# Cross-attention with image prompts: values projected with their weights standing, turned into row groups by VectorE, and some small work moved off VectorE

## The chip, the cores and the metric

The kernel runs on one core of a Trainium2 chip. The metric is the device time of one execution, in microseconds (us); lower is better. Engines are called as in the profile: PE is TensorE (matmuls; PEld its weight loads), DVE is VectorE, ACT is ScalarE, POOL is GpSimd, and SP is SyncE, which here only issues DMAs. All data is 32-bit floating point.

## What is computed

For each of 8 batches, 112 queries attend in 20 heads of 16 channels to a context of 371 text tokens and 4 image prompt tokens, each of 512 channels. The reference, cut to what matters (`heads` splits 320 channels into 20 heads of 16):

```python
q = heads(x @ W_q)                      # 8 x 20 x 112 x 16
k_t = heads(text @ W_k)                 # text: 371 tokens of 512
v_t = heads(text @ W_v)
probs_t = softmax(q @ k_t.T * 0.25)
text_out = probs_t @ v_t
k_ip, v_ip = heads(ip @ W_k_ip), heads(ip @ W_v_ip)   # 4 prompt tokens
qsem = l2norm(probs_t @ text)           # per head, 512 wide
sem = qsem @ l2norm(ip).T
probs_ip = softmax(q @ k_ip.T * 0.25 + 0.5 * sem) * spatial_mask
out = (text_out + probs_ip @ v_ip) @ W_out + b_out + x
```

The kernel never forms `qsem`. It forms the Gram matrix of the context (tokens by tokens, with the normalised prompts as further columns), and multiplies the exponentials of each head by a matrix `u` whose columns are the doubled upper half of that Gram matrix, the products with the prompts, a column of ones, and the 16 value channels of the head. One product thus gives the norm of `qsem`, the four similarities, the softmax's sum and the head's text output.

## The kernel before

The 20 heads are worked in 5 groups of 4; a step (b, g) is one group of one batch, and there are 40 steps. Group 0 to 3 take heads out of the first two chunks of 128 channels (a chunk holds 8 heads), group 4 the four heads of the last 64 channels. The four heads of a group lie in the four row groups of 32 partitions of TensorE, so that four small products run side by side.

In step n the main loop (lines 1253 to 1337) does the following, in an order written out by hand for TensorE, VectorE and SP throughout, and for ScalarE too in the main loop; GpSimd is ordered by the planner until near the end.
- `scores` (line 692) of the group two steps ahead (`LEAD = 2`): two heads at the start of the step, two behind the fifth block of the product. The scores go to two banks of PSUM (`ps_sc`, two buffers), so the later two need the banks of the earlier two. `maxima` (line 721, DVE) and `exponentials` (line 733, ACT, which for b > 0 also copies the four prompt logits, line 740) read them; `sent` (line 742) issues a DMA on SP that moves the probabilities of a head into the ring tile `xg`.
- `turned` (line 747): VectorE transposes `xg` of the next step in 32x32 blocks into `xgT`, in two pieces of 1024 and 512 elements.
- `multiplied` (line 760): the product of the current step, 12 blocks of 32 tokens times four heads, into four banks (`ps_qd`).
- `value_sums` (line 783, ACT) and `reduced` (line 815, DVE) read the four banks.
- `placed` (line 664, POOL) writes the values of the next step's heads into the value columns of `u`, from the tile `vr`.
- `between` (line 1113): pieces of other work that fill TensorE behind the product: `gram`, `values`, `keys`, `project_queries` for the coming batches, and `finish` of the last one (lines 836 to 960), which ends with the residual sum (line 955, DVE, out of PSUM) and the output DMA.

Values and keys of batch b + 1 are made during batch b. `values` (line 591) takes the context (`ctxT`, embedding by tokens) as the standing operand and the value weights as the moving one: three chunks of 128 tokens, each four matmuls of 320 columns, or of 384 for batches 1 to 6, where the 64 columns of the keys' third chunk are appended to the weights (line 1193). Each chunk is copied out by ScalarE into `vext` (tokens by channels). `regrouped` (line 614) then copies 16 blocks of 32 partitions into `vr`, whose row group a holds head a's values for all tokens; ScalarE and GpSimd do this in steps (b, 3) and (b, 4) (lines 1266 to 1270, 1324). `order_values` (line 252) has first put the weights' columns in the order that this needs. `keys` (line 546) keeps the weights standing and moves 371 columns of `ctxT` per chunk, which gives channels by tokens. The third chunk of keys is projected like that for batch 0 and, in `last_keys` (line 575), for batch 7, in step (7, 1); for batches 1 to 6 the 64 appended columns are spread by GpSimd (line 608) into `k3` and turned by three TensorE transposes (line 556) in step (b, 4). In the third chunk only every other block of 16 channels holds a head; the blocks between are zero (`spread`, line 139, does this to the weights).

`project_queries` (line 345) transposes x on VectorE, multiplies, and writes each chunk twice, times one of two masks that keep every other head (line 378): on VectorE, but for one chunk on ScalarE.

In the prologue (lines 1168 to 1217) the first context is transposed on TensorE (`transposed_context`, line 414, copied out by ScalarE, the second of three chunks by VectorE), the prompts are normalised on VectorE, and batch 0's keys and values, its first two groups' scores, the first chunk of batch 1's values and the loads of batch 2's context follow.

The last batch has a loop of its own (lines 1348 to 1405). In it GpSimd too is in written order: the bias sum of batch 6 (`with_bias`, line 832), which needs a load of x issued at the end of step (6, 4) (line 1230), stands ahead of `placed` for group 1.

Of the kernel before, what the change touches and what calls it, by code (L numbers as in the profile page):

```python
# [14 lines left out]
NIP = 4  # L15
# [5 lines left out]
def kernel(  # L21
# [83 lines left out]
    wv_sb = const.tile([P, NE, C + REST], F32, tag="wv_sb", name="wv_sb")  # L105
# [79 lines left out]
    wv_in = work.tile([P, BLK, P], F32, tag="xgT", name="wv_in")  # L185
    wv_in = wv_in.rearrange("p j k -> p (j k)")[:, : NE * C].rearrange("p (e f) -> p e f", f=C)
# [8 lines left out]
    load_embed(nc.sync, wv_in, w_v)  # L195
# [39 lines left out]
    k3 = const.tile([P, NT, GROUP, 2, D], F32, tag="k3", name="k3")  # L235

    def more_constants():
        nc.gpsimd.memset(k3[:, :, :, 1, :], 0.0)
# [6 lines left out]
    kip = const.tile([P, NC, N], F32, tag="kip", name="kip")  # L245
# [5 lines left out]

    def order_values():

        wv_by = wv_sb[:, :, :C].rearrange("p e (a g d) -> p e a g d", g=NG, d=D)
        for i in range(FULL):
            nc.vector.tensor_copy(
                wv_by[:, :, :, 2 * i : 2 * i + 2, :],
                wv_in[:, :, i * P : (i + 1) * P].rearrange("p e (a r d) -> p e a r d", r=2, d=D),
            )
        nc.vector.tensor_copy(  # L260
            wv_by[:, :, :, 2 * FULL, :],
            wv_in[:, :, FULL * P :].rearrange("p e (a d) -> p e a d", d=D),
        )
# [30 lines left out]
    def prompt_projections():  # L294

        both = work.tile([2 * N, CP], F32, tag="ipkv", name="ipkv", bufs=1)
        kp = both[:N]
        last = kp[:, FULL * P :].rearrange("n (a r d) -> n a r d", r=2, d=D)
# [28 lines left out]
        nc.scalar.copy(kip, ps[:, : NC * N].rearrange("p (i n) -> p i n", n=N))  # L327
        nc.gpsimd.tensor_copy(st[1]["kT"][:, :, TT:], kip[:, :, NIP : 2 * NIP])
        for i in range(NC):
            nc.gpsimd.tensor_tensor(  # L330
                kipb[:, i],
                kip[:, i, :NIP].unsqueeze(1).to_broadcast([P, HC, NIP]),
# [12 lines left out]
    def project_queries(bs):  # L345
# [16 lines left out]
        for i in range(NC):  # L362
# [13 lines left out]
            for r in range(2 if i < FULL else 1):  # L376
                by = nc.scalar.mul if (bs[0], i) == (1, 1) else nc.vector.tensor_scalar_mul
# [8 lines left out]
    def begin(b):  # L386
# [5 lines left out]
        s["kT"] = work.tile([P, NC, T], F32, tag="kT", name=f"kT_{b}")  # L392
        s["k3"] = k3
        s["u"] = work.tile([P, UCOL], F32, tag="u", name=f"u_{b}")
        s["vr"] = work.tile([P, BLK, NG, D], F32, tag="vr", name=f"vr_{b}")
# [1082 lines left out]
```

## Time and profile before

| | |
|---|---|
| time, median of 3 runs (lowest, highest) | 411.79 us (411.24, 412.38) |
| time of the profiled execution | 411.79 us |
| its span | 410.1 us |
| mean granted TensorE clock | 0.999 |
| busy ACT, POOL | 218.9 us (53%), 130.1 us (32%) |
| `ps_qd` matmuls, line 773 | 216.2 us, 3840 records |
| `ps_s`, line 702 | 65.3 us, 320 records |
| `ps_v`, line 599 | 63.1 us, 192 records |
| `ps_k`, line 565 | 46.6 us, 136 records |
| DVE transposes of probabilities, line 754 | 126.1 us, 79 |

A line of a timeline reads: start in us, duration in us, engine, line of the kernel, operation, output<-inputs by the program's names, shapes, and how many were merged (x2); in square brackets how long the engine had been idle ahead of it, and which instruction ended that. Merged pieces may overlap on the page, because an instruction's record is longer than the time until the next one starts. A line of the chain reads: start, us, engine, output tile, line, records. A matmul of 32-bit data leaves two records. A group's line reads: line, engine, operation, names and shapes, count, then busy us, mean ns of one, and the idle time ahead of the group with what ended it.

### The profile page before, as it was taken

The page shows a single profiled execution, that of the slowest core. Times are in us where ns is not written, and L with a number is a line of the kernel's source. Part 1 is how long each engine was busy: PE and PEld are TensorE (multiplying, and loading weights), DVE is VectorE, ACT ScalarE, POOL GpSimd, SP SyncE. Part 2 cuts the span into 40 slices and gives each one's busy share as a digit, 9 for nine tenths or more (in the row PEclk, how much of TensorE's full clock was granted, in tenths as well). Part 3 has the DMA queues.
Part 4 walks back from the last instruction along what each step waited for, and adds up shares of the span by engine and source line. Part 5 has one row for each costly group of instructions (what it writes and reads, how often), then busy time and mean ns, then how long its engine had stood idle before and what let it go on. Part 6 is the DMA issues. An engine that isn't in the chain of part 4 may idle for free.

```text
span 410.1 us, 14107 instructions
## 1 busy us (share of the span) xinstructions
PE 404.9 (99%) x5476; PEld 317.6 (77%) x5476; DVE 341.6 (83%) x734; ACT 218.9 (53%) x732; POOL 130.1 (32%) x321
## 2 busy tenths in 40 slices
PE   8999999999999999999999999999999999999996
PEld 7767777887778867888777877778777987787893
DVE  5667788897999979898899988889798977889775
ACT  2563345636375544646256363644537453678773
POOL 4842113021171204412052120702126121544640
PEclk9999999999999999999999999999999999999999
DMA  7575666548644555456554555545444356544300
GB/s 222 155 195 118 219 157 153 152 122 202 164 128 127 151 138 136 119 138 177 146 137 118 159 147 135 152 110 164 127 126 106 105 169 159 128 122 132 109 5 29
DMA packets 46435, 56.95 MB, mean 139 GB/s; under 512 B 9405, under 2 KB 40961, under 8 KB 46368
## 3 DMA queue, kind: packets, MB, share of 16 engines
q1 hardware_dynamic: 46328, 55.99, 51.3%
q8 instruction: 43, 0.70, 0.7%
q14 instruction: 24, 0.20, 0.2%
q10 hardware_dynamic: 40, 0.07, 0.1%
HBM read 15.88 MB, written 1.39 MB: 42 GB/s over the span
## 4 chain that ended last, share of the span: by engine, by line
PE 96%; DMA 1%; DVE 1%; issue 0%; ACT 0%; POOL 0%; SPq 0%; POOLq 0%
PE ps_qd L773 42%; PE ps_v L599 15%; PE ps_k L565 11%; PE ps_s L702 11%; PE ps_g L515 7%; PE ps_q L368 4%; PE ps_o L989 3%; DMA ct<-in_ctx_dram 1%; PE ps_g L471 1%; PE ps_o L944 1%; PE ps_k L581 1%; PE ps_k L556 0%; PE ps_a L977 0%; DVE ipnT L269 0%; PE ps_ipkv L306 0%
## 5 line engine op out<-in xcount | busy, mean ns | idle before, releaser
L773 PE MATMUL ps_qd<-u,xgT 32*112 32x168 f32 (+11 forms) x3840 | 216.2, 350 | 0.0
L773 PEld LDWEIGHTS ps_qd<-u,xgT 32*112 32x112 f32 x3840 | 184.4, 172 | 25.3 <-issue 0.5
L738 ACT ACTIVATE p<-ps_s,nmx 112x371 f32<-112x371 f32 x156 | 84.3, 578 | 81.5 <-DVE nmx L724 75.4
L754 DVE STREAM_TRANSPOSE xgT<-xg 128x512 f32<-128x512 f32 (+2 forms) x79 | 126.1, 1604 | 1.0 <-DMA ct<-in_ctx_dram 1.0
L724 DVE TENSOR_REDUCE nmx<-ps_s 112x1 f32<-112x371 f32 x160 | 78.8, 536 | 25.6 <-PE ps_s L702 24.4
L819 DVE CUSTOM_DVE_ANT_0 junk<-ps_qd,p 112x371 f32<-112x371 f32 x146 | 79.2, 543 | 19.1 <-ACT pvs L786 3.6
L671 POOL COPY u<-vr 128x64 f32<-128x64 f32 x120 | 26.4, 238 | 138.3 <-PE ps_qd L773 103.4
L702 PE MATMUL ps_s<-kT,qm 32*112 32x375 f32 (+1 forms) x320 | 65.3, 495 | 0.0
L599 PE MATMUL ps_v<-wv_sb,ctxT 128*128 128x384 f32 (+1 forms) x192 | 63.1, 477 | 0.0
L599 PEld LDWEIGHTS ps_v<-wv_sb,ctxT 128*128 128x128 f32 x192 | 35.7, 190 | 21.9 <-DVE qm L378 0.5
L565 PE MATMUL ps_k<-ctxT,wk_sb 128*128 128x371 f32 x136 | 46.6, 487 | 0.0
L702 PEld LDWEIGHTS ps_s<-kT,qm 32*112 32x112 f32 x320 | 25.4, 171 | 12.8 <-issue 10.3
L565 PEld LDWEIGHTS ps_k<-ctxT,wk_sb 128*128 128x128 f32 x136 | 24.5, 189 | 13.5 <-ACT vext L606 0.2
L619 ACT COPY vr<-vext 32x240 f32<-32x240 f32 x88 | 34.2, 389 | 1.3
L606 ACT COPY vext<-ps_v 128x384 f32<-128x384 f32 (+1 forms) x24 | 11.2, 467 | 41.3 <-PE ps_v L599 41.3
L515 PE MATMUL ps_g<-ctxT 128*32 128x375 f32 (+11 forms) x672 | 30.4, 333 | 0.0
L515 PEld LDWEIGHTS ps_g<-ctxT 128*32 128x32 f32 x672 | 27.7, 110 | 2.0
L422 DVE STREAM_TRANSPOSE ctxT<-ct 128x512 f32<-128x512 f32 x21 | 22.9, 1104 | 3.4 <-DMA ct<-in_ctx_dram 3.2
L964 POOL TENSOR_TENSOR wv<-vip,w 112x1280 f32<-112x1280 f32 x6 | 14.8, 2465 | 26.7 <-DVE w L902 26.7
L740 ACT COPY ipl<-ps_s 112x4 f32<-112x4 f32 x140 | 23.0, 164 | 0.0
L487 ACT ACTIVATE ug<-ps_g 128x375 f32<-128x375 f32 (+2 forms) x24 | 8.3, 375 | 24.1 <-PE ps_g L515 10.5
L488 POOL TENSOR_TENSOR ug<-ug,half 128x128 f32<-128x128 f32 (+1 forms) x24 | 10.4, 447 | 26.4 <-ACT ug L487 26.4
(171 smaller groups left out, 343.0 us busy)
## 6 DMA issues: line engine op xcount, KB each, us to landing
xg<-p SPq DMA_DIRECT2D x156, 162.3 KB
u<-ug SPq DMA_DIRECT2D x122, 99.0 KB
ct<-in_ctx_dram SPq DMA_DIRECT2D x28, 176.0 KB
vip<-vipd SPq DMA_DIRECT2D x6, 560.0 KB
xr_sb<-in_x_dram SPq DMA_DIRECT2D x32, 35.0 KB
out_dram<-ob SPq DMA_DIRECT2D x8, 140.0 KB
x_sb<-in_x_dram SPq DMA_DIRECT2D x6, 140.0 KB
xg<-wv_sb SPq DMA_DIRECT2D x4, 162.3 KB
```

The lines of the kernel that those rows point to most:

```text
L515: nc.tensor.matmul(ps[c][q * RG : (q + 1) * RG, j * RG - c * P : T - c * P], ctxT[:, e, j * RG : (j + 1) * RG], ctxT[:, e, j * RG : T], st ...
L565: nc.tensor.matmul(ps[:, :TT], wk_sb[:, e, i * P : (i + 1) * P], s["ctxT"][:, e, :TT], start=(e == 0), stop=(e == NE - 1),)
L599: nc.tensor.matmul(ps[:, :w], ctxT[:, e, c * P : (c + 1) * P], wv_sb[:, e, :w], start=(e == 0), stop=(e == NE - 1),)
L619: copy(s["vr"][a * RG : (a + 1) * RG, q::QN].rearrange("p c g d -> p c (g d)"), s["vext"][q * RG : (q + 1) * RG, :, a * w : (a + 1) * w],)
L671: nc.gpsimd.tensor_copy(v, dealt(b, c, s["vr"][:, c * QN : (c + 1) * QN, g, :]))
L702: nc.tensor.matmul(ps[:S, :w], qm[a * RG : (a + 1) * RG, i, r, j * S : (j + 1) * S], s["kT"][a * RG : (a + 1) * RG, i, :w], start=True, st ...
L724: nc.vector.tensor_reduce(nmx, s["sc", g, a][:S, :TT], AX.X, ALU.max, negate=True)
L738: nc.scalar.activation(s["p", g][:, a, :], ps[:S, :TT], AF.Exp, bias=nmx)
L740: nc.scalar.copy(s["ipl"][:, groups[g][a], :], ps[:S, TT:T])
L754: nc.vector.transpose(xT[:, j0:j1].rearrange("p j (k q) -> p q j k", q=QN), xg[:, :, j0 * RG : j1 * RG].rearrange("p q (j k) -> p q j k", ...
L773: nc.tensor.matmul(banks[a][:S, j * RG : UW], xT[a * RG : (a + 1) * RG, j, :S], region(b, c)[a * RG : (a + 1) * RG, q, j * RG - c * P :], ...
L819: nc.vector.tensor_tensor_reduce(out=junk, in0=ps[:S, :TT], in1=s["p", g][:, a, :], scale=1.0, scalar=0.0, op0=ALU.mult, op1=ALU.add, accu ...
```

## The change

- `values` now works as `keys` does: the value weights stand, 371 columns of context move, for the first two chunks of 128 channels. ScalarE copies a chunk into the new tile `vT` (channels by tokens).
- The value weights' last 64 columns go where the zeros stood in the keys' third chunk (`spread` with `other`); the third chunk is projected in full for every batch, and its rows hold keys and values in turn. The queries are zero in the rows of values, since their weights and masks are.
- `values_to_groups` has VectorE transpose a chunk in 32x32 blocks straight into `vr`: chunk 1 at the end of step (b, 0), the third chunk and the next batch's chunk 0 at the end of (b, 1); for batch 7 the third chunk and chunk 1 at the end of (6, 2) and (6, 3). `regrouped`, `order_values`, `k3`, the TensorE transposes of keys and `last_keys` are gone.
- `kT` has columns up to 384, and the prompts' keys `kip` are padded with zeros to 13 per batch.
- Batch 7's third chunk of keys moves from step (7, 1) to (6, 1), and one of its chunks of values from (6, 1) to (6, 2).
- The query masks go to ScalarE, except batch 0's and the last chunk of batch 7's. The residual of batches 0 to 5 becomes a ScalarE copy out of PSUM and a GpSimd sum.
- In the prologue the first context's copies are halved and all on ScalarE, the normalised prompts come one place later in part, and the loads of batch 2's context come earlier on SP.

```diff
-    wv_sb = const.tile([P, NE, C + REST], F32, tag="wv_sb", name="wv_sb")
+    wv_all = const.tile([P, NE * CP], F32, tag="wv_sb", name="wv_sb")
+    wv_sb = wv_all[:, : NE * C].rearrange("p (e f) -> p e f", f=C)
...
-    def spread(eng, t):
+    def spread(eng, t, other=None):
...
-        eng.memset(v[:, :, :, 1, :], 0.0)
+        if other is None:
+            eng.memset(v[:, :, :, 1, :], 0.0)
+        else:
+            eng.tensor_copy(
+                v[:, :, :, 1, :], other[:, :, FULL * P :].rearrange("p k (a d) -> p k a d", d=D)
+            )
...
+    vT = const.tile([P, FULL, TP], F32, tag="vT", name="vT")
+    nc.gpsimd.memset(vT[:, :, TT:], 0.0)
...
-                by = nc.scalar.mul if (bs[0], i) == (1, 1) else nc.vector.tensor_scalar_mul
+                by = nc.vector.tensor_scalar_mul
+                if qT is None and not (end and i == FULL):
+                    by = nc.scalar.mul
                 by(qm[:, i, r, : n * S], ps[:, : n * S], emask[:, r : r + 1])
...
+        n = NE // 2
         for c in range(NT):
...
+            for k in range(0, NE, n):
+                ps = bank(f"ps_c_{b}_{c}_{k}", spare=c == NT - 1)
+                for e in range(k, k + n):
...
+                nc.scalar.copy(
+                    ctxT[:, k : k + n, c * P : c * P + rows],
+                    ps[:, : n * P].rearrange("p (e t) -> p e t", t=P)[:, :, :rows],
                 )
...
+    def projected(ps, w, i, ctxT):
+
+        for e in range(NE):
+            nc.tensor.matmul(
+                ps[:, :TT],
+                w[:, e, i * P : (i + 1) * P],
+                ctxT[:, e, :TT],
+                start=(e == 0),
+                stop=(e == NE - 1),
+            )
+
     def keys(b):
...
+        for i in range(NC) if b < B - 1 else (FULL, 0, 1):
+            ps = bank(f"ps_k_{b}_{i}")
+            projected(ps, wk_sb, i, s["ctxT"])
             nc.scalar.copy(s["kT"][:, i, :TT], ps[:, :TT])
             yield
...
     def values(b):
...
+        for i in range(FULL):
+            ps = bank(f"ps_v_{b}_{i}")
+            projected(ps, wv_sb, i, st[b]["ctxT"])
+            nc.scalar.copy(vT[:, i, :TT], ps[:, :TT])
             yield
...
+    def values_to_groups(b, i):
+
+        src = vT[:, i] if i < FULL else st[b]["kT"][:, FULL]
+        nc.vector.transpose(
+            st[b]["vr"][:, :, 2 * i : 2 * i + 2].rearrange("p j r d -> p j (r d)"),
+            src.rearrange("p (j t) -> p j t", t=RG),
+        )
...
-        nc.vector.tensor_tensor(ob, s["o"][:S, :C], s["xb"], ALU.add)
+        if bd is None:
+            nc.scalar.copy(ob, s["o"][:S, :C])
+            eng.tensor_tensor(ob, ob, s["xb"], ALU.add)
+        else:
+            nc.vector.tensor_tensor(ob, s["o"][:S, :C], s["xb"], ALU.add)
...
         if g == 0:
+            values_to_groups(b, 1)
...
-            run(("v", nb), lambda: values(nb), 2)
+            run(("v", nb), lambda: values(nb), 2 if nb < B - 1 else 1)
+            if nb == B - 1:
+                run(("k", nb), lambda: keys(nb))
...
-            else:
-                run(("k", nb), lambda: keys(nb))
-            run(("v", nb), None)
+            run(("k", nb), lambda: keys(nb), 2 if 0 < b and nb < B - 1 else 1)
+            if nb == B - 1:
+                run(("v", nb), None)
...
+        if (b, g) in ((B - 2, 2), (B - 2, 3)):
+            values_to_groups(nb, FULL if g == 2 else 1)
+        if g == 1:
+            values_to_groups(b, FULL)
+            values_to_groups(nb, 0)
...
-            if nb < B - 1:
-                run(("k", nb), None, 1)
...
+    load_ctx_blocks(LEAD, rest=False)
     for a in range(GROUP):
         scores(0, 0, a, early=True)
         probabilities(0, 0, a)
...
-    load_ctx_blocks(LEAD, rest=False)
     spread(nc.gpsimd, wq_sb)
-    nc.gpsimd.tensor_copy(wv_sb[:, :, C:], wk_sb[:, :, FULL * P : C])
-    spread(nc.gpsimd, wk_sb)
+    spread(nc.gpsimd, wk_sb, wv_sb)
...
     drain(transposed_context(1))
+    values_to_groups(0, 0)
...
-                if g == 3:
-                    regrouped(b + 1, nc.gpsimd.tensor_copy, [(a, a) for a in range(GROUP)])
-                    regrouped(b + 1, nc.scalar.copy, across[0])
-                elif g == NG - 1:
-                    regrouped(b + 1, nc.scalar.copy, across[2])
...
-            regrouped(b + 1, nc.scalar.copy, across[1])
...
-            keys3 = last_keys(b, bank(f"ps_k_{b}_{FULL}", spare=True))
-            next(keys3)
-            next(keys3)
             run(("q", b), None)
```

More of the change, by code (lines that the diff above doesn't have):

```diff
@@ L548, in keys @@
         if b > 1:
[L549 to L571 removed]
+            nc.gpsimd.tensor_copy(s["kT"][:, :, TT:], kip[:, :, b])
@@ L1171 @@
     next(prompts)
-    next(context)
     next(products)
@@ L1175 @@
     next(context)
-    next(prompts)
+    next(context)
     run(("q", 0), lambda: project_queries(pairs[0]))
@@ L1200 @@
         probabilities(0, 1, a)
-    run(("v", 0), None)
+    run(("k", 0), None)
     run(("q", 0), None)
     drain(turned(0, 0, BLK))
-    for some in ([(a, a) for a in range(GROUP)], *across[1:]):
-        regrouped(0, nc.gpsimd.tensor_copy, some)
-    regrouped(0, nc.scalar.copy, across[0])
     grams_by(nc.scalar.copy, 0, [(a, QN - 1) for a in range(GROUP - 2)])
     placed(0, 0)
-    run(("k", 0), None)
+    load_ctx_blocks(LEAD, full=False)
     load_x_blocks(1, 0)
-    load_ctx_blocks(LEAD, full=False)
     load_x_blocks(2, 1)
```

124 lines of the change are left out of this document (21 added, 103 removed).

## The prediction

> **What bounds the kernel now.** I read the engine totals first, then the chain of work that ended last, then the busy time of steady steps, then the timelines of the engines around single waits. Step (b, g) is batch b, head group g.
>
> ```profile
> span 410.1 us, 14107 instructions
> ...
> PE 404.9 (99%) x5476; PEld 317.6 (77%) x5476; DVE 341.6 (83%) x734; ACT 218.9 (53%) x732; POOL 130.1 (32%) x321
> ```
> The chain, its pieces that belong to the two projections (start, us, what):
> ```profile
> 17.24 4.50 PE ps_v L599 x16
> ...
> 22.57 2.35 PE ps_v L599 x8
> ...
> 25.57 5.23 PE ps_k L565 x16
> ...
> 241.28 5.36 PE ps_v L599 x16
> ...
> 252.00 2.69 PE ps_k L565 x8
> 254.69 2.58 PE ps_v L599 x8
> ...
> 338.06 4.50 PE ps_v L599 x16
> ...
> 347.93 2.69 PE ps_k L565 x8
> 350.62 2.15 PE ps_v L599 x8
> ...
> 375.79 2.69 PE ps_k L581 x8
> ```
> and, in a narrower window of the same view, the transposes that turn the third chunk of keys:
> ```profile
> 321.87 0.32 PE ps_k L556 x3
> ```
> TensorE is the bound. That its rows fill the span proves little, since their ends are modelled; that time follows columns proves more: 16 records of 384 columns take 5.36, 16 of 320 take 4.50, so (5.36-4.50)/(16x64) = 0.84 ns per column, array time and no wait. The Trainium skill (Trainium Kernel Development and Optimization, Performance Expectations) warns that matmul busy time is a bad measure because matmuls are pipelined; by that alone the columns removed below could be worth nothing and the time would stay 411.8, but the scaling by columns speaks for their full price here.
>
> VectorE is second, and in places nearly full: the busy time by stretch, first for (1,3), then for (4,1) and (4,2), has it at 95%, 83% and 85% (columns: length; busy PE, PEld, DVE, ACT, POOL with counts; clock; DMA share; GB/s):
> ```profile
> 112.25:120.60 8.35, 8.35 (x119) 6.45 (x119) 7.92 (x17) 6.45 (x22) 7.94 (x14) 1.00 0.53 133
> ...
> 235.90:246.60 10.70, 10.70 (x126) 7.56 (x124) 8.83 (x17) 6.40 (x18) 2.17 (x6) 1.00 0.53 149
> 246.60:257.30 10.70, 10.70 (x125) 7.64 (x126) 9.10 (x23) 3.71 (x15) 1.28 (x5) 1.00 0.53 136
> ```
>
> **TensorE's part.** Values go from three chunks of 384 columns (320 for batches 0 and 7) to two of 371; the keys' third chunk, for batches 1 to 6 now three transposes, becomes a full chunk of 371. Two chunks in a row cost 5.23; a lone chunk of keys behind the attention product costs 2.69, and there is a second such one in each (b,3).
> Batches 1 to 6: before 5.36 + (2.69+2.58) + 2.69 + 0.32 = 13.64; after 5.23 + 5.23 + 2.69 = 13.15; saved 0.49 each, **2.9** in all.
> Batch 0, in the prologue: 4.50 + 2.35 becomes 5.23: **1.6** saved, keys unchanged. Ahead of that:
> ```profile
> L471 PEld LDWEIGHTS ps_g<-ctxT 128*128 128x128 f32 x48 | 5.8, 196 | 0.3 <-POOL ctxT L465 0.3
> ```
> The first context's transposes keep their count; their copies, in halves, all go to ScalarE, so VectorE reaches the normalised prompts sooner; TensorE's weight loads waited 0.3 there for them, and I take 0.2, between 0 and 0.3.
> Batch 7: before 4.50 + 2.69 + 2.15 + 2.69, and 2.69 in (7,1); after 5.23 + 5.23 + 2.69 and nothing in (7,1). So 1.1 is added ahead of the last batch, and 2.69 leaves it. What comes next there:
> ```profile
> 372.65 0.54 SPq L1220 DMA_DIRECT2D x_sb<-in_x_dram  x1
> ...
> 377.44 0.86 POOL L833 TENSOR_TENSOR xb<-x_sb,bias_sb 112x320 f32<-112x320 f32 x1 [4.91 <-DMA x_sb<-in_x_dram]
> 378.25 0.58 POOL L671 COPY u<-vr 128x64 f32<-128x64 f32 x3
> ...
> 379.06 2.32 PE L773 MATMUL ps_qd<-u,xgT 32*112 32x392 f32 x26
> ```
> The product of (7,1) needs the first of these three copies (done about 378.45), GpSimd runs them behind the bias sum, and that waits for the load of x. TensorE started at 379.06, only 0.6 later. The keys' chunk that goes is thus cover for the load: without it TensorE waits some 2.1 for what was hidden. Moreover batch 5's residual puts a copy on ScalarE (half a microsecond by rows further down) ahead of the exponentials and copies that free the banks of (7,0) for the query product. Of 2.69 I count **0.4** (0 to 2.69). Batch 7 costs 1.1 - 0.4 = 0.7.
>
> **VectorE's part.** Added: three 128x384 transposes per batch, 24 in all. No row has that shape; neighbours in a row are:
> ```profile
> 32.08 2.09 DVE L422 STREAM_TRANSPOSE ctxT<-ct 128x512 f32<-128x512 f32 x2 [3.23 <-DMA ct<-in_ctx_dram]
> ...
> 54.25 0.75 DVE L356 STREAM_TRANSPOSE xT<-xr_sb 128x128 f32<-128x128 f32 x3
> ```
> ```profile
> L754 DVE STREAM_TRANSPOSE xgT<-xg 128x512 f32<-128x512 f32 x35 | 39.3, 1124 | 0.0
> ```
> The first two give 1.045 for 512 elements and 0.25 for 128: 2.07 ns per element, so 0.78 for 384 (bounds 0.25 and 1.12, the mean of the dearest 512). 24 x 0.78 = 18.7. The Trainium skill (Vector Engine (DVE) Microarchitecture Reference, 3.8) has the transpose sustain one element per cycle and lane; with the 0.96 GHz of the Trainium skill (Trainium Kernel Development and Optimization, Quick Reference) that would be an estimated 0.40 for 384 and the stalls below would vanish (407.8). The rows show twice that, and they decide.
> Removed:
> ```profile
> L378 DVE TENSOR_SCALAR qm<-ps_q,emask 128x224 f32<-128x224 f32 x13 | 5.3, 443 | 1.9 <-PE ps_q L368 1.9
> L955 DVE TENSOR_TENSOR ob<-ps_o,xb 112x320 f32<-112x320 f32 x7 | 3.4, 483 | 0.0
> ```
> all 13 wide masks (5.3) and 6 of the 7 residuals (6 x 0.483 = 2.9), at least 8.2 without four narrow masks of batch 7 and the prologue's copies. So VectorE's net is at most +10.5, 352 of about 407. The total fits; the place matters. One transpose stands at the end of each step (b,0), two at the end of (b,1). There VectorE waited for TensorE before:
> ```profile
> 236.76 1.00 DVE L724 TENSOR_REDUCE nmx<-ps_s 112x1 f32<-112x371 f32 x2 [0.30 <-PE ps_s L702]
> ...
> 247.48 0.99 DVE L724 TENSOR_REDUCE nmx<-ps_s 112x1 f32<-112x371 f32 x2 [1.25 <-PE ps_s L702]
> ```
> The second transpose of (b,1) waits for ScalarE's copy of the first value chunk; that chunk is done a whole chunk (2.6) before the step ends, so this wait is covered by the ones ahead of it. After (b,0) the maxima come 0.78 - 0.30 = 0.48 late; some 0.05 of it is made good within (b,1), and behind (b,1) they are 0.43 + 1.56 - 1.25 = 0.74 late. Queued behind the maxima are the exponentials, and behind those TensorE: the later scores of a step reuse the banks that the earlier ones' exponentials and copies set free. In (4,2) and (1,3):
> ```profile
> 249.03 0.17 ACT L740 COPY ipl<-ps_s 112x4 f32<-112x4 f32 x1
> ...
> 250.13 0.48 PE L702 MATMUL ps_s<-kT,qm 32*112 32x375 f32 x2
> ```
> ```profile
> 113.39 0.94 DVE L724 TENSOR_REDUCE nmx<-ps_s 112x1 f32<-112x371 f32 x2
> ...
> 114.88 0.17 ACT L740 COPY ipl<-ps_s 112x4 f32<-112x4 f32 x1
> ...
> 115.75 0.48 PE L702 MATMUL ps_s<-kT,qm 32*112 32x375 f32 x2
> ```
> In (4,2) the bank came free at 249.20 and was wanted at 250.13, 0.93 of room; less 0.74, and less 0.13 by which TensorE is now earlier (5.36 - 5.23), 0.06 is left: no stall. In batches 1, 3 and 5 VectorE also turns x in (b,2), its maxima of (b,3) begin without a wait, and the whole lateness gets there: room 115.75 - 115.05 = 0.70 against 0.74 + 0.17. So a stall of 0.2 to 0.25 in each of the three: **0.7**, bounds 0 (a shorter transpose) and 5.75 (the 1.12 one, worked out below). A stall lets VectorE catch up by as much, so it isn't paid twice; and in (b,3) and (b,4) the masks and the residual that leave it undo the rest.
>
> **The other queues.** ScalarE and GpSimd lose the regrouping copies:
> ```profile
> L619 ACT COPY vr<-vext 32x240 f32<-32x240 f32 x88 | 34.2, 389 | 1.3
> ```
> ScalarE gains 17 masks and six copies of the output, both bounded by rows of its own:
> ```profile
> L804 ACT COPY shared<-ps_qd 112x371 f32<-112x371 f32 x11 | 5.1, 515 | 0.0
> ...
> L378 ACT ACTIVATE qm<-ps_q,emask 128x224 f32<-128x224 f32 x2 | 0.8, 444 | 0.7 <-PE ps_q L368 0.7
> ```
> At most 17 x 0.444 + 6 x 0.515 = 10.6, against 34.2 that go: cost taken 0, in the steps that have both. What is added is a wait: a mask on ScalarE waits for the query product, and the next step's first exponential is queued behind it. Two masks take 0.89 from the product's end; the maxima that the exponential needs anyway come about 1.0 after it (0.50 of scores and half of a 0.99 row of two), so they end last, and 0 to 0.4 is lost only where ScalarE is late already. GpSimd gains the residual's sum, 6 x 0.86 by row L833, at the end of (b,4), behind all three copies of values that the next product needs; taken at 0, and 0.86 per batch if it slipped in front of them.
> SP: four loads of batch 2's context move ahead of the first probabilities:
> ```profile
> 13.47 2.14 SPq L533 DMA_DIRECT2D u<-ug  x3
> ...
> 18.43 3.71 SPq L745 DMA_DIRECT2D xg<-p  x4
> ...
> 26.69 2.08 SPq L160 DMA_DIRECT2D ct<-in_ctx_dram  x4
> ```
> 2.08 of issue fits the hole from 15.6 to 18.4, and VectorE's wait of 3.23 for this load goes away. Cost taken: 0. If these loads held up the first probabilities or context sums in the queue, the prologue's 1.8 would be lost; that is the bound.
>
> **Sum.** 2.9 + 1.6 + 0.2 - 0.7 - 0.7 = 3.3. The profiled execution took 411.79, with 1.7 outside its span, and equals the median; 411.79 - 3.3 = **408.5**.
>
> **Rivals.**
> 1. Everything comes through: no stall, and the last batch gives its 2.69: 2.9 + 1.6 + 0.2 + 1.6 = 6.3, **405.5**. For it: TensorE's unbroken chain; against: GpSimd's wait of 4.91.
> 2. VectorE takes over as the bound, slower: the transposes cost 1.12 like the dearest 512. Each batch's scores in (b,2) or (b,3) then come 3 x 0.34 = 1.0 later, with no room left: 3 x 1.25 + 2 x 1.0 = 5.75 stalled in batches 1 to 5 instead of 0.7, **413.5**. Without stalls the gain is 3.3 + 0.7 = 4.0, and 15 transposes carry the lateness: 0.7 + 15 x (t - 0.78) reaches 4.0 at t = 1.0, and 5.2, which is measurably slower, at t = 1.08: from there this mechanism decides. For it: (1,3) has no idle VectorE; against: the rate is steady from 128 to 512 elements.
> 3. The same at 1.0 per transpose, or columns of TensorE that turn out to be no array time: the change ends where it began, **411.8**.
> 4. The prologue gives nothing, because the moved load delays what the first product waits for: 3.3 - 1.8 = 1.5, **410.3**.
>
> **How the numbers follow.** Forecast 0.50 (407 to 410), rival 1 0.15, rival 2 0.17, rival 3 0.10, rival 4 0.08. 0.3% is 1.2 us, about the least that a measurement of this kernel tells from none: faster ends at 410.6. Faster: 0.47 + 0.15 + 0.06 = 0.68; slower: rival 2 and a rest, 0.18; within: 0.14. The range reaches from just under rival 1 to between rivals 3 and 2: 405.3 to 412.8, leaving out some 0.05 below and 0.13 above.
>
> **What would show it.** Right: 128 records of values instead of 192 and 192 of keys, two chunks in a row near 5.23; the new 128x384 transposes near 0.8; the maxima after (b,1) without a wait for TensorE; first product of batch 0 some 1.8 earlier; in the last batch a gap or stretched query product ahead of (7,1) with GpSimd still waiting for x. Wrong: transposes over 1.0; score rows of TensorE late by more than 0.5 in even batches; (7,1) starting right behind its query product.

## The result and the profile after

| | before | after |
|---|---|---|
| median, us | 411.57 (20 runs, 410.94 to 413.42) | 410.78 (20 runs, 409.62 to 411.82) |
| profiled execution: time, span | 411.79, 410.1 | 410.67, 409.0 |
| mean granted TensorE clock, profiled | 0.999 | 0.989 |

The ratio of the times is 0.9977 (95% interval 0.9967 to 0.9988): 0.8 us faster. That is clear of noise, and yet within the 0.3% that the prediction called no change. Forecast were 408.5 and a gain of 3.3: the range, 405.3 to 412.8, held the time, but only a quarter of the forecast gain came.

The profile's page after the change: the span, the engine totals, and of the 40 slices TensorE's busy tenths and the granted clock.
```profile
span 409.0 us, 13891 instructions
...
PE 400.4 (98%) x5442; PEld 314.2 (77%) x5442; DVE 340.3 (83%) x731; ACT 191.7 (47%) x663; POOL 118.3 (29%) x282
...
PE   9999999999999999999999999999999999996996
...
PEclk9999999999999999999999999999999999997999
```
TensorE is busy 4.5 less, though the span shrank by 1.1 only. VectorE has the share that it had, ScalarE and GpSimd are relieved by 27 and 12. New are a 6 in TensorE's row and a 7 in the clock's, in slice 37 (368 to 378). The chain of work that ended last shows the projections (start, us, what):
```profile
92.98 5.18 PE ps_v L547 x16
...
103.53 5.18 PE ps_k L547 x16
...
114.08 2.69 PE ps_k L547 x8
```
These are the five chunks that one batch needs, two in a row at 5.18. So the change does what it says. Where the time went is read from four marks on TensorE's timeline: the first scores of the main loop, the product of step (7,0), the last query product, and the first transpose of the closing work. Before (start, us, engine line, operation, count):
```profile
33.31 0.57 PE L702 MATMUL ps_s<-kT,qm 32*112 32x371 f32 x2
...
370.11 1.22 PE L773 MATMUL ps_qd<-u,xgT 32*112 32x392 f32 x10
...
378.31 0.82 PE L368 MATMUL ps_q<-xT,wq_sb 128*128 128x112 f32 x6
...
398.61 0.29 PE L908 MATMUL ps_wT<-ident,w 112*80 112x112 f32 x1
```
and after, the idle time ahead of an instruction and what ended it in brackets:
```profile
30.57 0.57 PE L658 MATMUL ps_s<-kT,qm 32*112 32x371 f32 x2
...
364.88 1.22 PE L729 MATMUL ps_qd<-u,xgT 32*112 32x392 f32 x10
...
374.01 1.63 PE L363 MATMUL ps_q<-xT,wq_sb 128*128 128x112 f32 x6 [3.50 <-ACT shared L760]
...
397.16 0.29 PE L864 MATMUL ps_wT<-ident,w 112*80 112x112 f32 x1
```
Subtracting mark from mark:

| stretch | before | after | difference | forecast |
|---|---|---|---|---|
| prologue, to the first scores | 33.31 | 30.57 | -2.74 | -1.8 |
| steps up to (7,0) | 336.80 | 334.31 | -2.49 | -1.1 (-2.9 + 0.7 + 1.1) |
| (7,0) to the last query product | 8.20 | 9.13 | +0.93 | -0.4, with the next row |
| query product to the closing work | 20.30 | 23.15 | +2.85 | |
| closing work to the span's end | 11.49 | 11.84 | +0.35 | 0 |
| span | 410.1 | 409.0 | -1.1 | -3.3 |

At (7,0) the kernel is 5.2 ahead, more than forecast. The last batch gives 4.1 of it back, and most of that behind the query product, where the work is the same as before. (The 0.35 of the closing work is for the most part a wait for GpSimd, 0.5 in place of 0.2 in the profiles' lists of TensorE's waits.) The other engines show how the wait of 3.50 came about. With the change:
```profile
364.99 0.43 ACT L912 COPY ob<-ps_o 112x320 f32<-112x320 f32 x1 [0.41 <-PE ps_o L949]
...
365.50 0.86 POOL L913 TENSOR_TENSOR ob<-ob,xb 112x320 f32<-112x320 f32 x1 [4.30 <-ACT ob L912]
...
370.88 0.86 POOL L789 TENSOR_TENSOR xb<-x_sb,bias_sb 112x320 f32<-112x320 f32 x1 [1.96 <-DMA x_sb<-in_x_dram]
```
and the chain behind that residual sum, down to the copy that ends TensorE's wait at 374.01:
```profile
366.36 1.87 POOL shared L764 x2
...
368.25 0.61 ACT shared L768 x2
...
368.88 0.03 DVE rn L830
...
369.06 1.52 DVE xgT L710
...
371.84 0.49 DVE nmx L680
...
372.36 0.57 ACT wv_sb L694
...
373.59 0.38 ACT shared L760
```
Before, GpSimd went straight to the shared sums (the products of `shared` and `p`) of (6,4):
```profile
369.57 1.90 POOL L808 TENSOR_TENSOR shared<-shared,p 112x371 f32<-112x371 f32 x2 [2.34 <-ACT shared L804]
```
GpSimd now idles 4.30 until ScalarE's copy of batch 5's output is done, adds the residual, and only then multiplies the shared sums of (6,4). Against the product of (7,0) they start 1.44 after it (366.32, 364.88), where they started 0.54 ahead of it before (369.57, 370.11): 1.98 later. From there the chain runs through ScalarE and VectorE, whose turning and maxima come behind the sums, to the exponentials and the copies of (7,0), the last of which frees the bank for the query product. And while TensorE waits its clock falls. The busy time by stretch, TensorE alone (busy, granted clock, DMA share, GB/s):
```profile
372.00:373.00 1.00, 0.00 (x0) 1.00 0.00 0
373.00:374.00 1.00, 0.00 (x0) 0.52 0.38 83
...
378.00:379.00 1.00, 1.00 (x12) 0.50 0.00 0
...
379.50:380.00 0.50, 0.50 (x11) 0.63 0.00 0
```
From 373.0 to 379.9 it is 0.50, also for 5.9 us in which TensorE is busy again; half of that is 2.9, near the 2.85 of the table. Not only in this execution: in all 20 the mean granted clock of the span lies between 0.989 and 0.996; the kernel before had 0.999 in its profiled execution, and 0.997 to 1.000 in the runs beside the experiments below.

### The profile page after: what moved, and what is told of

It reads as the page before. It is cut to its first block, busy times and chain, and to the rows that moved or that the text cites. A ratio compares the mean times of both kernels' runs of the same rounds, so it can differ in the third digit from the quotient of the medians.

```text
span 409.0 us, 13891 instructions
## 1 busy us (share of the span) xinstructions
PE 400.4 (98%) x5442; PEld 314.2 (77%) x5442; DVE 340.3 (83%) x731; ACT 191.7 (47%) x663; POOL 118.3 (29%) x282
## 4 chain that ended last, share of the span: by engine, by line
PE 96%; ACT 1%; issue 1%; POOL 1%; DVE 1%; POOLq 0%; DVEq 0%
PE ps_qd L729 41%; PE ps_k L547 15%; PE ps_s L658 11%; PE ps_v L547 10%; PE ps_g L513 7%; PE ps_q L363 4%; PE ps_o L949 3%; PE ps_g L469 1%; PE ps_w L448 1%; PE ps_o L900 1%; POOL shared L764 0%; PE ps_a L937 0%; DVE xgT L710 0%; PE ps_c L432 0%; PE ps_ipkv L298 0%
## 5 line engine op out<-in xcount | busy, mean ns | idle before, releaser
L547 PE MATMUL ps_k<-ctxT,wk_sb 128*128 128x371 f32 x192 | 64.6, 484 | 0.0
L547 PEld LDWEIGHTS ps_k<-ctxT,wk_sb 128*128 128x128 f32 x192 | 35.1, 190 | 20.3 <-ACT vT L569 0.5
L547 PE MATMUL ps_v<-ctxT,wv_sb 128*128 128x371 f32 x128 | 42.4, 482 | 0.0
L547 PEld LDWEIGHTS ps_v<-ctxT,wv_sb 128*128 128x128 f32 x128 | 23.7, 190 | 14.5 <-issue 0.5
L562 ACT COPY kT<-ps_k 128x371 f32<-128x371 f32 x24 | 11.2, 468 | 37.8 <-PE ps_k L547 37.8
L363 PE MATMUL ps_q<-xT,wq_sb 128*128 128x224 f32 (+1 forms) x90 | 17.5, 335 | 3.5 <-ACT shared L760 3.5
L569 ACT COPY vT<-ps_v 128x371 f32<-128x371 f32 x16 | 7.5, 468 | 25.4 <-PE ps_v L547 25.4
```

Source lines behind the costliest of these rows:

```text
L363: nc.tensor.matmul(ps[:, : n * S], wq_sb[:, j, i * P : (i + 1) * P], xT[:, j, :n, :, : S // QN], start=(j == 0), stop=(j == NC - 1),)
L547: nc.tensor.matmul(ps[:, :TT], w[:, e, i * P : (i + 1) * P], ctxT[:, e, :TT], start=(e == 0), stop=(e == NE - 1),)
```

## The experiments

Theory T: the last batch took the gain back by two things that hang together, a longer wait for the query product (the residual stands in the way, and the keys' chunk that covered the rest has gone), and a clock that falls for it. The runs of the kernel before that were made beside each of the following had medians of 411.4 to 411.5, so medians of different sessions are compared; the changed kernel is taken at 410.8.

**Batch 5's residual back on VectorE**, the rest as changed:
```
-        if bd is None:
+        if bd is None and b < B - 3:
             nc.scalar.copy(ob, s["o"][:S, :C])
```


> Only batch 5's residual goes back to VectorE; all else as in the changed kernel (410.8). Theory T (batch 5's residual stands on ScalarE and GpSimd ahead of the prompts' weights of step (6,4), the query product comes 2.0 us later for it, TensorE idles 3.5 us, and the granted clock then falls to 0.5 for some 5 us, which costs 3.1): the idle time falls to about 1.5, the clock stays at 1.00, 4 to 5 us less, about 406.2. Rival S (the idle time costs, the slow queries after it are not the clock's doing): 2.0 less, about 408.8. Rival X (the load of x and its sum with the bias hold (7,1) anyway): 410.8.

Measured: 406.94, ratio 0.9893 (0.9875 to 0.9910), 3.8 less than with the change, where T had 4 to 5 and rival S 2.0. In the profiled execution, which at 408.1 was the slowest of five:
```profile
372.50 1.24 PE L363 MATMUL ps_q<-xT,wq_sb 128*128 128x112 f32 x6 [1.95 <-ACT shared L760]
```
```profile
372.00:373.00 1.00, 0.49 (x4) 0.98 0.66 178
373.00:374.00 1.00, 1.00 (x8) 0.50 0.63 177
...
376.00:377.00 1.00, 1.00 (x16) 0.82 0.01 3
```
The wait falls from 3.50 to 1.95, where T had 1.5, though the load of x was left as it was: the load is not the gate, and rival X is out. One thing T had not: the clock could fall at 1.95 too, here for some 3.4 us. In two of the five runs its mean was 0.996 or less (408.0 and 408.1), in three 0.998 to 1.000 (406.7 to 406.9): 1.3 us between them, a first price of a shorter fall.

**TensorE kept busy, nothing waiting less:**
```
         if g == 1:
+            projected(bank("ps_fill", spare=True), wk_sb, FULL, st[b]["ctxT"])
             run(("q", b), None)
```


> The changed kernel with six matmuls more (the third key chunk of batch 7 a second time, result unused, 2.7 us) ahead of the last query product: nothing waits less, TensorE is only kept busy through most of the idle 3.5 us. Theory T: the clock stays at 1.00 and the 3.1 us of the slow queries are saved, about 407.7. Rival S: no gain, 410.8 or a little more. Rival X: 410.8.

Measured: 408.40, ratio 0.9923 (0.9909 to 0.9936). Work that nobody needs makes the kernel 2.4 us faster. (The chunk is four matmul calls, eight instructions in the trace, not six as the expectation has it.)
```profile
371.17 2.76 PE L547 MATMUL ps_fill<-ctxT,wk_sb 128*128 128x371 f32 x8 [0.81 <-ACT ipl L696]
373.91 0.92 PE L363 MATMUL ps_q<-xT,wq_sb 128*128 128x112 f32 x6
...
394.24 0.30 PE L864 MATMUL ps_wT<-ident,w 112*80 112x112 f32 x1
```
The query product starts at 373.91, practically when it did (374.01); but then it takes 0.92 in place of 1.63, and the mean clock was 0.998 to 1.000 in all runs. From the query product to the closing work it takes 20.33, as in the kernel before (20.30), and not 23.15. So the slow instructions behind the wait were the clock's doing, all of the 2.85, and rival S is out. (By the medians it is 2.4 where T had 3.1. In 5 of the 20 runs with the change the mean clock was 0.996, in the others 0.989 to 0.992, so the fall was not equally long in all of them.)

**Batch 7's third key chunk back ahead of the last query product**, the turning of its values with it:
```
-        for i in range(NC) if b < B - 1 else (FULL, 0, 1):
+        for i in range(NC if b < B - 1 else FULL):
...
         if g == 1:
+            ps = bank(f"ps_k_{b}_{FULL}", spare=True)
+            projected(ps, wk_sb, FULL, st[b]["ctxT"])
+            nc.scalar.copy(st[b]["kT"][:, FULL, :TT], ps[:, :TT])
+            values_to_groups(b, FULL)
             run(("q", b), None)
```


> The third key chunk of batch 7 (and the turning of its values to row groups) goes back from step (6,1) to just ahead of the last query product, where the kernel before had it. Theory T: 2.7 us of TensorE's work leave the full stretch and stand in the idle 3.5 us, and the clock does not fall: 2.7 + 3.1 less, about 405.0. Rival S: 2.7 less, 408.1. Rival X: 408.1 too, since the stretch ahead gets shorter only if x is not the gate: between 408.1 and 410.8.

Measured: 407.68, ratio 0.9903 (0.9887 to 0.9918): 3.1 less, where T expected 5.8. The clock was held (0.998 to 1.000), but the chunk does not give its 2.6 there. (With the third chunk gone from (6,1), the other chunks of batch 7 move up by one place, and the place that comes free is the last, in (6,3).) Step (6,4), from its query product to the product of (7,0), becomes longer:
```profile
353.71 0.83 PE L363 MATMUL ps_q<-xT,wq_sb 128*128 128x112 f32 x6
...
363.77 1.22 PE L729 MATMUL ps_qd<-u,xgT 32*112 32x392 f32 x10
```
10.06 against 356.34 to 364.88, 8.54, with the change: 1.5 of the 2.6 is lost. And behind the query product it takes 20.86 (372.91 to 393.77) where 20.30 was to be had. What (6,4) waits for is read behind the next kernel, which has the same step.

**Both together,** the two edits above that move the residual and the chunk back:

> Both: batch 5's residual on VectorE and batch 7's third key chunk ahead of the last query product. Theory T: no idle time of more than half a microsecond left there and the clock at 1.00: 3.5 + 3.1 less at most, less up to 1.2 that the key chunk takes beyond the idle time left: 404.2 to 405.4. Rival S: 407.3. Rival X: 408.1 or more.

Measured: 406.00, ratio 0.9862 (0.9847 to 0.9876), the fastest of the study, though 0.6 above what T's upper bound said. TensorE's waits are all of a few tenths but for the start (engine, line, what it waited for: total, times, longest):
```profile
PE ps_w L448 <- PEq L1415: 0.8, 1, 0.8
PE ps_a L1012 <- POOL attn L1003: 0.5, 1, 0.5
```
The wait ahead of the last query product has gone. What T overlooked is again (6,4). VectorE's maxima at the start of that step, with the change:
```profile
358.02 1.90 DVE L680 TENSOR_REDUCE nmx<-ps_s 112x1 f32<-112x371 f32 x4 [0.86 <-PE ps_s L658]
```
and with the chunk late (the kernel of the experiment above, where no residual is on VectorE):
```profile
356.99 1.85 DVE L680 TENSOR_REDUCE nmx<-ps_s 112x1 f32<-112x371 f32 x4
```
With the change VectorE waits 0.86 for TensorE's scores; with the chunk late it comes straight from the turning of values and does not wait. In that step it is busy for 9.53 of 10.10, in both kernels with the late chunk, against 7.60 of 8.60 with the change. So 2.6 of TensorE's work was taken away ahead of a step in which VectorE was only 0.86 ahead, and VectorE is the limit there. This is read from the rows, it was not tried apart.

The four kernels together give what one part costs with and without the other:

| | third key chunk late | third key chunk early |
|---|---|---|
| batch 5's residual on VectorE | 406.0 | 406.9 |
| on ScalarE and GpSimd | 407.7 | 410.8 |

The residual costs 1.7 where the chunk covers it and 3.8 where not; the earlier chunk costs 0.9 or 3.1.

**The residuals alone, in the kernel before:**
```
-        nc.vector.tensor_tensor(ob, s["o"][:S, :C], s["xb"], ALU.add)
+        if bd is None:
+            nc.scalar.copy(ob, s["o"][:S, :C])
+            eng.tensor_tensor(ob, ob, s["xb"], ALU.add)
+        else:
+            nc.vector.tensor_tensor(ob, s["o"][:S, :C], s["xb"], ALU.add)
```


> The kernel before (411.5) with one part of the change alone: the residuals of batches 0 to 5 on ScalarE and GpSimd. There the bank for the last query product came free at 377.63, 0.85 ahead of the end of the third key chunk (378.48) that TensorE worked on meanwhile. Theory T (the residual delays that bank by 1.5 to 2.0, and what is not covered by the key chunk is idle time; the clock holds as the gap is short): 0.7 to 1.1 more, about 412.4, clock 1.00. Rival S (each part of the change costs the same with or without the other): at least 3.8 more, what giving the residual of batch 5 back to VectorE saved, 415.3. Rival N (the residual costs nothing while the chunk is there): 411.5.

Measured: 412.91, ratio 1.0049 (1.0035 to 1.0062): 1.5 more, between T's 0.7 to 1.1 and rival S's 3.8, and much nearer T. The clock stayed at 0.998 to 1.000.
```profile
377.87 2.76 PE L581 MATMUL ps_k<-ctxT,wk_sb 128*128 128x371 f32 x8 [0.75 <-ACT ipl L740]
...
380.59 0.92 PE L368 MATMUL ps_q<-xT,wq_sb 128*128 128x112 f32 x6
```
T had the place wrong by one instruction: not the query product comes late but the key chunk ahead of it, whose bank the late exponentials of (7,0) free. From the product of (7,0), at 371.44 here, to the query product it takes 9.15 against 8.20: 0.95. From there to the closing work (401.46) it takes 20.87 against 20.30: 0.57. The two make the 1.5; why the 0.57 is lost was not followed up. The steps from the first scores (34.66) to (7,0) take 336.78 against 336.80, so the five residuals there cost nothing. The profiled execution, with 414.66 the slowest of six, has its further 1.35 ahead of the first scores, where TensorE waited 1.59 for VectorE's part of `order_values`.

**All residuals on VectorE**, chunk late (`if False:` in place of `if bd is None:`), to see whether the other five matter:

> All seven residuals on VectorE as before the change (0.48 each, one per batch), batch 7's third key chunk ahead of the last query product; else the changed kernel. Against 406.0 with only batch 5's residual there. If the residuals of batches 0 to 4 on ScalarE and GpSimd cost something in the steady steps (the kernel before lost 1.5 with the moved residuals where the gap in the last batch explains 0.9): 405.4 or less. If VectorE is short of room in the steady steps, 0.5 for each of up to five batches: up to 408.4. Theory R (neither): 406.0, within 0.4.

Measured: 406.14, ratio 0.9869 (0.9849 to 0.9888), against 406.00: neither. Moving the five residuals of the steady batches was worth nothing; moving the sixth cost 1.7 or 3.8, by the table above.

**Every turning of values twice** (`for _ in range(2):` around the transpose), to see how much room VectorE had. First what one turning took with the change (columns as in the page's groups: busy, mean ns, idle before):
```profile
L575 DVE STREAM_TRANSPOSE vr<-vT 128x384 f32<-128x384 f32 x16 | 8.9, 553 | 0.0
...
L575 DVE STREAM_TRANSPOSE vr<-kT 128x384 f32<-128x384 f32 x8 | 4.4, 549 | 0.0
```


> The changed kernel (410.8) with each turning of values into row groups done twice, 24 x 0.55 = 13.2 us more on VectorE, so that one turning costs 1.10, the price of the prediction's second rival (1.12). By that rival, VectorE stalls TensorE by about 5.75 in batches 1 to 5: 416.5. Theory R (VectorE has room at these places, lateness runs out within the step): at most 1.0 more, 410.8 to 411.8.

Measured: 417.42, ratio 1.0136 (1.0114 to 1.0158), 6.6 more than with the change. Theory R falls, and the prediction's second rival, written for a turning of 1.12, holds nearly to the size. The first products of steps (4,1), (4,2) and (4,3), with the change:
```profile
230.80 0.58 PE L729 MATMUL ps_qd<-u,xgT 32*112 32x392 f32 x2
241.35 0.58 PE L729 MATMUL ps_qd<-u,xgT 32*112 32x392 f32 x2
251.89 0.58 PE L729 MATMUL ps_qd<-u,xgT 32*112 32x392 f32 x2
```
and with each turning done twice:
```profile
235.62 0.58 PE L730 MATMUL ps_qd<-u,xgT 32*112 32x392 f32 x2
246.17 0.58 PE L730 MATMUL ps_qd<-u,xgT 32*112 32x392 f32 x2
257.65 0.58 PE L730 MATMUL ps_qd<-u,xgT 32*112 32x392 f32 x2
```
Step (4,1) keeps its 10.55, step (4,2) goes from 10.54 to 11.48. All of the 0.94 stands in the step behind the two turnings of (b,1), where the prediction put it, with 1.0. Read in the same way, batch 2 loses 0.94 too, and batches 1 and 3 lose 1.26 and 1.23, a part of it in (b,3), where the second rival had 1.25. Batch 5 loses 2.28, which the rival did not have. (This profiled execution, with 418.64 the slowest of five, is 8.0 above that of the changed kernel.) At 0.55 a turning there is no stall, at twice that about a microsecond in each of batches 1 to 4.

**Masks back on VectorE**, in the fastest kernel (`if (bs[0], i) == (1, 1):` as before the change):

> The best kernel so far (406.0: batch 5's residual on VectorE, batch 7's third key chunk late) with the masks back on VectorE, 13 wide ones of about 0.4, 5.3 us in all, at most two per step. Doubling the turnings (13.2 us) cost 6.6, so VectorE has no room to give after steps (b,1). Theory V (room is short wherever VectorE gets more ahead of the maxima): 1 to 3 more, 407 to 409. Theory R (the masks fall in steps (b,2) to (b,4), apart from the turnings, and are hidden): 406.0 to 406.4.

Measured: 406.74, ratio 0.9878 (0.9859 to 0.9896), 0.7 above the fastest kernel. That lies between the two theories; the intervals of the two ratios overlap. In the profiled executions two steps are longer, (4,0) by 0.33 (9.96 against 9.63) and (7,0) by 0.32 (9.27 against 8.95), and the rest are the same within 0.02; but ahead of (4,0) VectorE also idles 1.00, which is no time of the masks. So a small cost is likely but not settled.

**The prologue, order of context and prompts as before:**
```
     next(context)
     next(prompts)
+    next(context)
     next(products)
     next(prompts)
     next(context)
-    next(context)
+    next(prompts)
     run(("q", 0), lambda: project_queries(pairs[0]))
```


> The changed kernel with the prologue's order of context and prompts as in the kernel before: second context block ahead of the first sums of products, prompts earlier. The first main product came 2.75 earlier with the change, of which 1.6 are the values with weights standing; 1.1 came ahead of the first query product. Theory O (the order gave these 1.1: TensorE does the first block's products while it would wait for the second block's load and for VectorE's prompts): first main product at about 31.7, 1.1 more, 411.9. Rival C (the context copies in halves on ScalarE gave them): 410.8.

Measured: 410.56, ratio 0.9985 (0.9976 to 0.9993), the same as with the change; the first query product came at 11.45 in place of 11.26. Theory O falls, as long as the copies are in halves.

**The prologue, context copied block by block as before**, one copy of four on VectorE:
```
-                nc.scalar.copy(
+                (nc.vector.tensor_copy if c == 1 else nc.scalar.copy)(
                     ctxT[:, k : k + n, c * P : c * P + rows],
```
with `n = NE` and no spare bank.

> The changed kernel with the prologue's context copied a block at a time, the second block by VectorE, as in the kernel before; the order of the changed kernel stays. Theory O: 0 to 0.3 more, 410.8 to 411.1, first main product at 30.6 to 30.9. Rival C (the halves on ScalarE gave the 1.1): first main product at about 31.7, 411.9.

Measured: 411.65, ratio 1.0014 (0.9997 to 1.0031): 0.9 more, rival C. TensorE's rows, start of the products of the context:
```profile
5.38 1.16 PE L469 MATMUL ps_g<-ctxT 128*128 128x128 f32 x8 [0.68 <-ACT ctxT L437]
...
8.59 4.72 PE L469 MATMUL ps_g<-ctxT 128*128 128x128 f32 x40 [1.10 <-DVE ctxT L437]
```
With the copies in halves the first wait was 0.16 and the second did not exist. The first query product came at 13.15, later than in the kernel before (12.43), which has whole copies too but the old order. So the halves are worth 1.89 in the new order (13.15 to 11.26); in the old it is 0.98 (12.43 to 11.45), though more than the copies differs between those two kernels. Whether it is the halves or the engine of the one copy was not tried apart. The first scores came at 32.46, 1.9 after those of the changed kernel, more than rival C's 1.1. The medians differ by 0.9 only, and here the clock hides a part:
```profile
376.40 1.10 PE L363 MATMUL ps_q<-xT,wq_sb 128*128 128x112 f32 x6 [3.52 <-ACT shared L760]
```
The wait is the same as with the change, but in this execution the clock was 0.50 from 377.0 to 380.4 only, and from the query product to the closing work (398.36) it took 21.96 in place of 23.15. Among runs of a mean clock of 0.996 the two kernels differ by 1.2 (means of 411.4 and 410.2).

**Half the filling**, in two kernels, to see what makes the clock fall. The first, with a loop over four matmul calls:

> The changed kernel with four matmuls (1.35 us, result unused) ahead of the last query product in place of eight: the idle 3.5 us are cut into about 0.8 ahead of them and 1.3 behind them. If the length of the longest gap decides over the clock: clock 1.00 in all runs, 408.4 as with eight. If the idle share of a stretch decides: clock below 0.998 in some runs, with times between 408.4 and 410.8. Rival S is out already.

Measured: 408.58, ratio 0.9926 (0.9910 to 0.9942). This was a miss: a chunk is four calls, so it was the full filling once more, and it only repeats that result. The second, with two calls:
```
         if g == 1:
+            ps = bank("ps_fill", spare=True)
+            for e in range(2):
+                nc.tensor.matmul(
+                    ps[:, :TT], wk_sb[:, e, FULL * P :], st[b]["ctxT"][:, e, :TT], start=(e == 0), stop=(e == 1)
+                )
```


> The changed kernel with half of the idle time's filling: two calls (about 1.4 us, result unused) ahead of the last query product in place of four calls (2.7 us). The idle 3.5 us are cut into about 0.8 ahead of them and 1.4 behind them, 2.2 in all; with batch 5's residual on VectorE there was one gap of 1.95, and the clock stood below 0.997 in two of five runs. If the length of the longest gap decides over the clock: 0.998 or more in all runs, 408.5 as with the whole filling. If the idle time within a stretch decides: below 0.997 in two or more of the runs, and these 1.2 or more longer. Rival G (any gap over 1 us costs the clock): below 0.997 in all, about 410.

Measured: 408.57, ratio 0.9931 (0.9918 to 0.9945). Five executions had a clock of 0.999 or 1.000 and 408.4 to 408.7; the profiled one had 0.989 and took 412.44:
```profile
372.20 1.51 PE L1306 MATMUL ps_fill<-ctxT,wk_sb 128*128 128x371 f32 x4 [0.81 <-ACT ipl L696]
374.93 1.62 PE L363 MATMUL ps_q<-xT,wq_sb 128*128 128x112 f32 x6 [1.21 <-ACT shared L760]
```
```profile
375.00:376.00 1.00, 1.00 (x5) 0.50 0.66 190
...
381.00:382.00 1.00, 1.00 (x14) 0.73 0.00 0
```
No gap here is longer than 1.21, and yet the clock was 0.50 from about 374.7 to 381.5. The longest gap alone does not decide. That idle time within a stretch does, in an execution that falls unluckily, agrees with this one and with the 1.95 above; but two or more such runs were expected and there was one, so the rule is not settled.

## Why the prediction was right and wrong

- **Batches 1 to 6, "saved 0.49 each, 2.9".** Right, and a little small: two value or two key chunks in a row took 5.18, not 5.23, so 13.64 becomes 13.05 and 0.59 each, 3.5 in all. Batch 7's "1.1 is added ahead of the last batch" is 12.03 to 13.05, 1.0; 3.5 - 1.0 is the 2.49 of the table.
- **VectorE, "0.78 for 384" and stalls of "0.7".** The mechanism was right, only the size was off: a turning takes 0.55, and no step of batches 1 to 5 is longer than before. The line through the rows of 128 and 512 elements overshot by 0.23, and against rival 2 the prediction had called that rate steady. The estimate from the Trainium skill (Vector Engine (DVE) Microarchitecture Reference, 3.8), 0.40, that the prediction set aside was too low by 0.15, but its consequence, no stalls, was what happened. Done twice, the turnings stall batches 1 to 4 nearly as the second rival said.
- **Batch 0, "1.6 saved".** Right: from the first query product to the first scores it went from 20.88 (12.43 to 33.31) to 19.31 (11.26 to 30.57). **The prompts, "I take 0.2, between 0 and 0.3"**, were mis-sized: the first query product comes 1.17 earlier. The prediction read the wait of the weight loads on the prompts alone; the copies in halves on ScalarE also take away waits ahead of it, 0.68 and 1.10 in the run with whole copies, whose first query product came 1.89 later.
- **Batch 7, "Of 2.69 I count 0.4".** This is the step that failed. The prediction saw that the key chunk was cover, and saw the copy that batch 5's residual puts on ScalarE. But it named the load of x as what comes next, and it took "GpSimd's residual sum" at 0 because it stands "behind all three copies of values that the next product needs", and never asked what stands behind it: the shared sums of (6,4), on whose path lies the bank of the last query product. The 0.86 that the prediction held ready for such a slip was too small as well, since the sum also waits for ScalarE's copy: the shared sums start 1.98 later. The load of x did not set the time: with the residual alone given back, the wait fell from 3.50 to 1.95. The query product is late by 0.93, where the whole last batch was to be 0.4 faster.
- **The clock** is in no term of the prediction, and it is the larger half of the miss: the wait of 3.50 costs 2.85 more than itself, as the filling shows. The prediction's list did name the sign, "a gap or stretched query product ahead of (7,1)"; it read it as a wait, not as a clock.

In sum the prologue gave 0.9 and the steps 1.4 more than forecast, 2.3 together, and the last batch came out 4.5 worse (4.1 in place of -0.4): 3.3 + 2.3 - 4.5 is the 1.1 of the profiled executions, 0.8 by the medians. That the time still fell into the range is luck: errors of 2.3 and 4.5 went opposite ways. With one line undone (batch 5's residual) the kernel has 406.9, and with the chunk late too 406.0, 5.5 less than before.

## What to carry to other kernels

Before work that covers a wait is moved away, find what the wait really ends on by following its bank back through every queue, and look what each moved instruction now stands ahead of, not only what it stands behind. A gap on TensorE is to be priced with the clock that may fall behind it; filling the gap with work that nobody needs tells the two apart in one run. An operation that is moved off a busy engine in every iteration can be free in all of them but the last.

## What the hardware showed that was not expected

- In this case the granted clock fell to half on idle times of TensorE shorter than 3 us. The Trainium skill (TensorE: Matmul & The Clock Gate, Why this matters for your kernels) says to leave no idle gaps over about 3 us between bursts. The gap of 3.50 agrees, with a fall in 20 of 20 executions, judged by the mean clock; but one of 1.95 made it fall in two of five, and gaps of 0.81 and 1.21 in one of six. The same page (What's actually happening) has a free-running window of 3413 ns; the falls here lasted about 3.4 (373.0 to 376.4) and 6.8 or 6.9 (373.0 to 379.9, 374.7 to 381.5), one and two such windows, which agrees.
- The same wait of 3.5 had falls of either length, 6.8 with the change and 3.4 with whole copies. In the six profiled executions with a fall, it was the long one where the clock fell while TensorE still waited (the change: fall at 373.0, work again at 374.01; the half filling: 374.7 and 374.93; the doubled turnings and the old order likewise), and the short one where TensorE was at work again by then (batch 5's residual back: work at 372.50, fall at 373.0; whole copies: 376.40 and 377.0). In the 3.4 us ahead of each fall that the document shows, TensorE had idled 1.8 to 2.8 in all; in profiled executions without a fall it idled 0.75 (the late chunk) and 0.81 (the filling). This is a pattern in a few executions, not a tested rule.
- What it costs, from the query product to the closing work, where the work is the same: 20.33 without a fall (the filling), 21.96 with a short one, 23.15 and 23.51 with a long one. Between whole executions it was 1.3 for the short fall (batch 5's residual back), 2.4 for the filling, and 3.9 for the one execution of the half filling against the other five.
- A 128x384 turning takes 0.55, so 1.43 ns per element, where the prediction's rows of 128 and 512 elements gave 1.95 and 2.04, and the page after the change has 2.05 us for a 128x1024 transpose of probabilities, 2.00 ns per element. Why 128x384 is cheaper was not tried.
